# A graph attention layer on one core: pick units that run on across groups, and reciprocals that follow their roots later

## The chip, the cores and the metric

The kernel runs on one core of one Trainium2 chip. The metric is the device time of one execution in microseconds. The kernel before took 2001.13 us in the median of 3 runs, 1995.0 to 2002.62 us.

Five engines work beside each other, each in the order of its own instruction stream, and they wait for one another by semaphores: TensorE (PE in the profile, its weight loads PEld), VectorE (DVE), ScalarE (ACT), GpSimd (POOL) and SyncE (SP). Here GpSimd only issues gathers and SyncE only issues the other DMAs.

## The reference

6250 nodes with 64 features, 206250 directed edges sorted by destination. For each edge the key and value rows of its source and the query row of its destination meet with a projection of the edge's own features; messages are summed by destination, added to x, and normalised.

```python
Qh = (x @ Wq.T + bq).reshape(n, H, D)
Kh = (x @ Wk.T + bk).reshape(n, H, D)
Vh = (x @ Wv.T + bv).reshape(n, H, D)
Ee = (edge_attr @ We.T + be).reshape(-1, H, D)
score = (Kh[src] * Qh[dst] * (1.0 / np.sqrt(D)) * Ee).sum(-1)
score = jnp.exp(jnp.clip(score, -5.0, 5.0))
msg = Vh[src] * score[..., None]
wV = jax.ops.segment_sum(msg, dst, num_segments=n)
x = _layernorm(x + wV)
```

H is 4, D is 16.

## The kernel before

Edges come in 1612 tiles of 128. Eight tiles are a **group** (1024 edges); there are 202 groups, and the main loop (L1014) runs over them. Two groups are a **step**; sums of a step are made in the even group that follows it (L1079), so only every second group has them, and they are added (`add`, L893) in the odd group after that.

A group g needs five things of its neighbours in the pipeline: `edges` (L746) projects the edge features of g+3 into the PSUM tile `room`, first half; `biased` (L751) copies that to `eb` on ScalarE with the bias; `queries` (L757) spreads query rows over edges by a one-hot matrix `to` into the PSUM tile `qq`; `terms` (L765) multiplies the two on VectorE; `turn` (L771) transposes the product into `qe` on TensorE. Then `products`, `weigh` and `message` (L804, L811, L817) make scores, weights and messages, `keep` and `take` (L842, L846) split a message into two parts (`msg`), and `sums` (L865) multiplies them on TensorE with the one-hot `wide` (made by `onehot_edges`, L777, on VectorE as `of` and widened on ScalarE). The sums land in the second half of `room`.

**Where keys and values come from.** Most tiles get their rows by indirect DMA on GpSimd (`gather`, L316, one tile each). Some are picked by TensorE instead: four tiles (512 sources) are one **collection** m. A collection is 13 **units**; a unit is four matmuls of 128x512 (the last unit two) of node features `parts` with a one-hot matrix `hot`, summed in two PSUM tiles `pick` (`picks`, L709). Units come in 7 **pieces** of two (the last of one); `hots` (L688) makes the one-hot of a piece on VectorE one group ahead, pieces 1, 3 and 5 as `thin` in bf16, which ScalarE widens (L707). When the 13 units are done, `picked` (L719) reads both `pick` tiles on VectorE into `x` (L722, L723). Only then may the next collection's first unit overwrite `pick`. In the group after, `biased_kv` (L731, ScalarE) puts a bias into `qq`, `picked_kv` (L725) makes 16 matmuls on it, `place_kv` (L736, ScalarE) copies the rows out, and only after this copy can `queries` write `qq` again. `sources` (L254) prepares the next collection's indices with two ScalarE passes and one on VectorE; `fetch_sources` (L248) loads them.

Collections take 3 and 2 groups by turns. The group in which a collection ends is in `READY` (3, 5, 8, 10, 13, ...), the one in which it begins in `BEGIN`. A collection never shares a group with another: a three-group collection runs 4, 4 and 5 units, a two-group one 6 and 7. The order of all instructions is written out by hand, the loop body being that order.

At the end of blocks of 128 nodes, `roots` (L978, ScalarE: a table of functions is loaded, then a square root), `scales` (L981, VectorE: the reciprocal) and `norm` (L984) follow each other in one group, for batches that close at 16, 32, 42 and 47 blocks.

Of the kernel before, what the change touches and what calls it, by code (L numbers as in the profile page):

```python
# [97 lines left out]


def pieces_of(g):  # L100

    for m in range(LAST):
        if BEGIN[m] <= g <= READY[m]:
            n, k = READY[m] - BEGIN[m] + 1, g - BEGIN[m]
            return [(m, p) for p in range(len(PIECES) * k // n, len(PIECES) * (k + 1) // n)]
    return []

# [42 lines left out]
def tile_gnn(ctx: ExitStack, tc: tile.TileContext, x, x_blocks, by_rows, xT, wT, bias, beT, weT, eT, src, src_rows,  # L150
# [502 lines left out]
    with tc.If(rv == 0) as branch:  # L653

        with tc.tile_pool(name="work", bufs=2) as work, \
# [13 lines left out]
            folded = room[:, 1, 2 * PA:2 * PA + 2 * C].rearrange("p (b c) -> p b c", c=C)  # L669
            sum_ = still[:, 2 * P:2 * P + C]  # L670
# [310 lines left out]
            def scales(lo, hi):  # L981
                nc.vector.reciprocal(rstd[:, lo:hi], rstd[:, lo:hi])
# [12 lines left out]

            closed, scaled, normed = 0, 0, 0
            step_of = {g: s for s in range(NS) for g in groups_of(s)}
# [16 lines left out]
            for g in range(NG + 1):  # L1014
                now, before = g < NG, g > 0
                todo, ahead = [(m, p, u) for m, p in pieces_of(g) for u in range(*PIECES[p])], pieces_of(g + 1)
                going, where = [], []
# [8 lines left out]
                if g % LG == 0 and g + 3 * LG < NG:  # L1026
                    fetch_edges(g // LG + 3, work, 3)
                if g + 1 in BEGIN[1:]:
                    fetch_sources(BEGIN.index(g + 1) + 1, work)
                if g + 4 < NG:  # L1030
# [48 lines left out]
                if g - 1 in ends and now:  # L1079
# [3 lines left out]
                    else:  # L1083
                        short.append(lambda: sums(s))
                for k in range(max(len(todo), 3)):
# [11 lines left out]
                    if k in (2, 4) and short and g not in READY:  # L1097
# [5 lines left out]
                if g + 3 < NG:  # L1103
# [19 lines left out]
                if parted:  # L1123
                    take(g, 0)
                if g in READY:
                    picked(READY.index(g))
                if done:

                    while closed < B - 2 and summed[closed] <= g:
                        spreads(closed)  # L1130
                        closed += 1
                    if closed in BATCHES and closed > scaled:
                        roots(scaled, closed)
                        scales(scaled, closed)
                        scaled = closed
                    for _ in range(3):
# [185 lines left out]
```

## Time and profile before

The profiled execution took 2019.47 us, 18.3 us over the median of the runs; its span, from the first to the last instruction, is 2017.7 us.

| What | Before |
|---|---|
| median of 3 runs | 2001.13 us |
| profiled execution | 2019.47 us |
| its span | 2017.7 us |
| granted TensorE clock, mean | 0.932 |
| TensorE busy | 1738.5 us |
| VectorE busy | 1486.0 us |
| ScalarE busy | 1328.1 us |
| GpSimd busy | 1255.5 us |

A row of the groups reads: line, engine, operation, written tile and read tiles, shape, count, then busy time in all, mean ns of one, and the idle time of the engine just before these instructions with what ended it. A row of the waits reads: who waited, for whom, us in all, how often, the longest. A row of the timeline reads: start, duration, engine, line, instruction, and in brackets the idle time before it and what ended it. A row of the windows lists for a stretch the busy time of each engine and then the share of full speed that the TensorE clock was granted (PEclk). All of TensorE's products are recorded at one helper line, L744, so tiles tell them apart.

### The profile page before, as it was taken

To read this page: it belongs to the slowest core of one execution; us is meant where nothing else is said; L and a number is where in the kernel's file an instruction comes from. 1 tells how busy PE (TensorE), PEld (TensorE's weight loads), DVE (VectorE), ACT (ScalarE), POOL (GpSimd) and SP (SyncE) were. 2 spreads that over 40 slices of the span, in tenths; PEclk is the share of its full clock that TensorE was granted. 3 is DMA by queue.
4 is the path that set the end of the run, shared out by engine and by line. 5 is a ranking of instruction groups with operands and counts; after the bars stand their busy time and mean duration, and the time that the engine had idled before them with its cause. 6 is when DMAs were issued, how large, how long until landed. Compare 5 with 4: busy or idle time off the path is not lost.

```text
span 2017.7 us, 25692 instructions
## 1 busy us (share of the span) xinstructions
PE 1738.5 (86%) x7993; PEld 1259.1 (62%) x7993; DVE 1486.0 (74%) x2650; ACT 1328.1 (66%) x2047; POOL 1255.5 (62%) x1310
## 2 busy tenths in 40 slices
PE   6569989888888898979888989888888988889995
PEld 6346666666666665657566666666666666656664
DVE  5457777777777686878777777778777777678786
ACT  3456676676766676767667667667766667577674
POOL 6566666666666665666666666666666666666441
PEclk9789999999999998999899999999989999999996
DMA  6523333333333333333333333333333333333320
GB/s 178 190 90 114 100 103 103 98 97 100 93 108 101 91 102 88 102 115 99 93 97 92 107 104 93 104 90 103 101 88 114 104 95 104 97 93 98 97 71 20
DMA packets 116116, 203.70 MB, mean 101 GB/s; under 512 B 54784, under 2 KB 56425, under 8 KB 115855
## 3 DMA queue, kind: packets, MB, share of 16 engines
q1 hardware_dynamic: 73932, 116.94, 19.0%
q0 software_dynamic: 41600, 83.97, 14.7%
q10 hardware_dynamic: 436, 1.04, 0.2%
q8 instruction: 65, 1.06, 0.2%
q14 instruction: 83, 0.68, 0.1%
HBM read 194.25 MB, written 7.59 MB: 100 GB/s over the span
## 4 chain that ended last, share of the span: by engine, by line
PE 63%; DVE 16%; issue 7%; ACT 6%; another core or an unknown queue 4%; DMA 2%; POOL 1%; DVEq 0%; SPq 0%; ACTq 0%; POOLq 0%
PE pick L744 37%; PE room L744 10%; PE qq L744 10%; PE qe L775 4%; DVE hot L696 3%; DMA kv<-kv_tab,src_i 2%; DVE score L808 2%; DVE prod L806 1%; DVE qe L830 1%; DVE x L722 1%; DVE term L769 1%; POOL kv L295 1%; ACT kv L739 1%; DVE msg L850 1%
## 5 line engine op out<-in xcount | busy, mean ns | idle before, releaser
L295 POOL DMA_INDIRECT kv<-kv_tab,src_i x1260 | 1216.2, 965 | 708.8 <-issue 277.1
L744 PE MATMUL pick<-hot,parts 128*128 128x512 f32 x3900 | 1143.6, 436 | 115.5 <-DVE x L722 79.5
L744 PEld LDWEIGHTS pick<-hot,parts 128*128 128x128 f32 x3900 | 742.3, 198 | 418.8 <-issue 167.8
L696 DVE TENSOR_TENSOR hot<-from,still 128x1024 fp32r<-128x1024 bf16 x231 | 280.3, 1213 | 0.6 <-ACT from L257 0.6
L707 ACT ACTIVATE hot<-thin 128x1024 fp32r<-128x1024 bf16 x234 | 245.4, 1049 | 19.4 <-remote 19.3
L769 DVE TENSOR_TENSOR term<-eb,qq 128x512 f32<-128x512 f32 x202 | 137.3, 680 | 137.2 <-PE qq L744 98.1
L755 ACT ACTIVATE eb<-room,be_col 128x512 f32<-128x512 f32 x202 | 137.1, 679 | 148.2 <-DVE still L900 50.4
L744 PE MATMUL room<-et,we_sb 128*128 128x512 f32 x404 | 226.2, 642 | 7.5 <-ACT eb L755 6.2
L844 ACT ACTIVATE msg<-qe 128x512 fp32r<-128x512 f32 (+1 forms) x206 | 123.2, 598 | 157.5 <-DVE qe L830 74.4
L278 ACT ACTIVATE to<-to,one_p 126x1024 bf16<-126x1024 bf16 x198 | 225.7, 1140 | 0.1
L272 ACT ACTIVATE to<-kb,minus_row 126x1024 bf16<-126x1024 uint8 x198 | 225.2, 1137 | 0.0
L813 ACT ACTIVATE score<-score,five_p 128x32 f32<-128x32 f32 x203 | 64.1, 316 | 235.4 <-DVE score L808 144.6
L775 PE MATMUL qe<-ident,term 128*128 128x128 f32 x806 | 135.5, 294 | 58.9 <-DVE term L769 39.4
L775 PEld LDWEIGHTS qe<-ident,term 128*128 128x128 f32 x806 | 104.0, 151 | 111.9 <-DVE term L769 55.8
L744 PE MATMUL qq<-w,x 128*128 128x128 f32 x1248 | 165.8, 288 | 5.0 <-issue 3.6
L806 DVE TENSOR_TENSOR prod<-kv,qe 128x512 f32<-128x512 f32 x203 | 137.0, 675 | 43.1 <-remote 38.3
L830 DVE SCALAR_TENSOR_TENSOR qe<-weight,kv 128x512 f32<-128x512 f32 x200 | 139.8, 699 | 35.1 <-ACT weight L815 22.3
L722 DVE SCALAR_TENSOR_TENSOR x<-odd,upper,pick 128x512 f32<-128x512 int32 x77 | 57.3, 744 | 144.7 <-PE pick L744 115.2
L744 PEld LDWEIGHTS qq<-w,x 128*128 128x128 f32 x1248 | 155.6, 202 | 12.9 <-issue 8.0
L696 DVE TENSOR_TENSOR thin<-from,still 128x1024 bf16<-128x1024 bf16 x231 | 157.1, 680 | 0.0
L808 DVE TENSOR_REDUCE score<-prod 128x32 f32<-128x512 f32 x203 | 138.5, 682 | 7.0
L850 DVE TENSOR_TENSOR msg<-qe,msg 128x512 fp32r<-128x512 f32 x194 | 132.2, 681 | 2.9 <-ACT msg L844 1.4
(166 smaller groups left out, 1490.5 us busy)
## 6 DMA issues: line engine op xcount, KB each, us to landing
et<-in_eT SPq DMA_DIRECT2D x100, 512.0 KB
kb<-key_tab SPq DMA_DIRECT2D x101, 252.0 KB
kv<-kv_tab,src_i POOLq DMA_INDIRECT x1260
srcs<-in_src_rows SPq DMA_DIRECT2D x78, 256.0 KB
qw<-q_tab SPq DMA_DIRECT2D x202, 15.8 KB
kv_tab<-kv_sb SPq DMA_DIRECT2D x4, 640.0 KB
q_tab<-q SPq DMA_DIRECT2D x5, 480.0 KB
out<-y SPq DMA_DIRECT2D x2, 512.0 KB
```

Source lines behind the costliest of these rows:

```text
L272: nc.scalar.activation(TO[g][:, :n, :], KB.pop(g)[:, :n * P].rearrange("p (j e) -> p j e", j=n), AF.Square, bias=minus_row3[:3 * W])
L278: nc.scalar.activation(TO[g][:, :n, :], TO[g][:, :n, :], AF.Relu, bias=one_p[:3 * W], scale=-1.0)
L295: return nc.gpsimd.indirect_dma_start(out=kv_of(g)[:, j, :], out_offset=None, in_=kv_tab[:, :], in_offset=bass.IndirectOffsetOnAxis(ap=src ...
L696: nc.vector.tensor_tensor(to.rearrange("p b (a c) -> p b a c", c=2), pairs((FROM if hi < UNITS else OVER)[m])[:, None].to_broadcast(shape) ...
L707: nc.scalar.activation(*THIN.pop(0), AF.Copy)
L744: mark.append(nc.tensor.matmul(*aps, **kw))
L769: nc.vector.tensor_mul(TERM[g][:, :n], EB.pop(g)[:, :n], qq[:, :n])
L775: nc.tensor.transpose(qe[g % 2][:, 2 * k:2 * k + 2, :], TERM[g][:, k, :], ident)
L806: nc.vector.tensor_mul(prod, kv_of(g)[:, lo:hi, :C], qe[g % 2][:, lo:hi, :])
L808: nc.vector.tensor_reduce(SCORE[g], prod.rearrange("p g (h d) -> p g h d", h=H), axis=AX.X, op=OP.add)
L830: nc.vector.scalar_tensor_tensor(to.rearrange("p g (h d) -> p g h d", h=H), WEIGHT.pop(g)[:, :, :, None].to_broadcast([P, n, H, D]), LEAST ...
L850: nc.vector.tensor_sub(part_of(g, 1)[1], left, part)
```

## The change

Three things change, and the arithmetic stays the same.

1. All units of all collections are one stream, and groups take 4, 6, 6, 4, 6 units of it by turns (5 in the very first). A collection's last units now share a group with the next one's first: in a group of `READY` the **head** is what still belongs to the ending collection. It has 2 units in groups 3, 8, 13, ... (short head) and 5 in groups 5, 10, 15, ... (long head). With a short head, head and `picked` come early in the group, ahead of the one-hots; then `turn`, `queries`, `sums` and `edges`, and behind them 4 units of the next collection. With a long head, the head comes where units stood before, then `queries`, `sums`, `edges`, and behind them one unit of the next collection; `picked` stands ahead of `onehot_edges`. `sources` moves from the group after into the group of `READY`, and `fetch_sources` from the group of `READY` into the one before.
2. The PSUM tile `room` of two halves becomes two tiles: `ee` (for `edges`) and `room` (for `sums` and the folding of blocks).
3. `scales` of a batch follows `roots` two groups later (the last batch at once, as before).

```diff
+FLOW = 4, 6, 6, 4, 6
+STREAM = [(m, p, u) for m in range(LAST) for p, piece in enumerate(PIECES) for u in range(*piece)]
+UPTO = [0] * (LEAD + 1)
+for g in range(LEAD, NG):
+    UPTO.append(UPTO[-1] + FLOW[(g - LEAD) % len(FLOW)] + (g == LEAD))
...
+def units_of(g):
+
+    return STREAM[UPTO[g]:UPTO[g + 1]] if g < NG else []
...
 def pieces_of(g):
...
+    return [(m, p) for m, p, u in units_of(g) if u == PIECES[p][0]]
...
+SOURCES = {LEAD: 1, **{r: m + 2 for m, r in enumerate(READY)}}
+FETCHES = {r - 1: m + 2 for m, r in enumerate(READY)}
...
-            room = fixed.tile([P, 2, 4 * P], F32, name="room")
-            ee = room[:, 0].rearrange("p (i e) -> p i e", e=P)
-            pa = room[:, 1, :2 * PA]
+            ee = fixed.tile([P, G // 2, P], F32, name="ee")
+            room = fixed.tile([P, 4 * P], F32, name="room")
+            pa = room[:, :2 * PA]
...
+                todo, ahead = units_of(g), pieces_of(g + 1)
+                ending = READY.index(g) if g in READY else None
+                head = [one for one in todo if one[0] == ending]
...
+                if 0 < len(head) <= 3:
+                    for one in head:
+                        picks(*one)
+                        where.append(mark[-1])
+                    picked(ending)
...
+                for k, one in enumerate(head if len(head) > 3 else []):
+                    picks(*one)
+                    where.append(mark[-1])
+                    if k == 1 and g + 1 < NG:
+                        turn(g + 1)
+                if head:
+                    if len(head) <= 3 and g + 1 < NG:
+                        turn(g + 1)
+                    if g + 2 < NG:
+                        queries(g + 2)
+                    while short:
+                        short.pop(0)()
+                    if g + 3 < NG:
+                        edges(g + 3)
+                    if len(head) > 3:
+                        picked(ending)
+                    for one in todo[len(head):]:
+                        picks(*one)
+                        where.append(mark[-1])
+                for k in range(0 if head else max(len(todo), 3)):
...
-                if g in BEGIN:
-                    sources(BEGIN.index(g) + 1, *from_odd())
+                if g in SOURCES:
+                    sources(SOURCES[g], *from_odd())
...
-                if g in READY:
-                    picked(READY.index(g))
...
+                    if rooted > scaled:
+                        scales(scaled, rooted)
+                        scaled = rooted
+                    if closed in BATCHES and closed > rooted:
+                        roots(rooted, closed)
+                        rooted = closed
+                        if closed == BATCHES[-1]:
+                            scales(scaled, closed)
+                            scaled = closed
```

Three places of the built programs show it, all around group 13, a group with a short head. First TensorE, at the end of group 13 before: the last unit (two single matmuls), the edge features of group 16, and the next collection's first unit.

```order
L744 MATMUL pick_757<-hot,parts 128x512
L744 MATMUL pick_758<-hot,parts 128x512
L744 MATMUL room<-et,we_sb 128x512
L744 MATMUL pick_757<-hot,parts 128x512 x2
L744 MATMUL pick_758<-hot,parts 128x512 x2
```

And TensorE from the last unit on in the changed program; the two `pick` tiles are called pick_758 and pick_759 there.

```order
L758 MATMUL pick_758<-hot,parts 128x512
L758 MATMUL pick_759<-hot,parts 128x512
L789 MATMUL qe_763<-ident,term 128x128 x4
L758 LDWEIGHTS qw
L758 MATMUL qq<-to,qw 64x512
L758 LDWEIGHTS qw
L758 MATMUL qq<-to,qw 64x512
L758 MATMUL ee<-et,we_sb 128x512
L758 MATMUL pick_758<-hot,parts 128x512 x2
L758 MATMUL pick_759<-hot,parts 128x512 x2
```

Between the last unit of one collection and the first of the next stood `edges` alone; now `turn` (`qe`), `queries` (`qq`) and `edges` stand there.

Second VectorE in group 13 before, from the first one-hot ahead to `picked` (the two `x`); `of` is the one-hot of the sums, `msg` is `take`.

```order
L696 TENSOR_TENSOR hot<-from,still 128x1024
L830 SCALAR_TENSOR_TENSOR qe_763<-weight,kv_67 128x512
L696 TENSOR_TENSOR thin<-from,still 128x1024
L696 TENSOR_TENSOR hot<-from,still 128x1024
L792 TENSOR_TENSOR of<-still,key 128x1024
L850 TENSOR_TENSOR msg<-qe_763,msg 128x8x64
L722 SCALAR_TENSOR_TENSOR x_759<-odd,upper,pick_757 128x512
L723 SCALAR_TENSOR_TENSOR x_760<-odd,upper_82,pick_758 128x512
```

And VectorE in group 13 of the changed program:

```order
L736 SCALAR_TENSOR_TENSOR x_760<-odd,upper,pick_758 128x512
L737 SCALAR_TENSOR_TENSOR x_761<-odd,upper_82,pick_759 128x512
L710 TENSOR_TENSOR hot<-from,still 128x1024
L844 SCALAR_TENSOR_TENSOR qe_764<-weight,kv_67 128x512
L710 TENSOR_TENSOR thin<-from,still 128x1024
L273 TENSOR_SCALAR odd<-srcs 128x512
L806 TENSOR_TENSOR of<-still,key 128x1024
L864 TENSOR_TENSOR msg<-qe_764,msg 128x8x64
```

`picked` has moved from the end of the group to ahead of the first one-hot and of the message (L844); one one-hot has gone to another group and `odd` (of `sources`) has come.

Third ScalarE, with what each instruction waits for, from `biased` (`eb`) of group 13 to `biased_kv` of group 14 (the `qq` row), before:

```order
L755 ACTIVATE eb<-room,be_col 128x512 [waits DVE_49,PE_49]
L844 ACTIVATE msg<-qe_763 128x8x64 [waits DVE_49]
L272 ACTIVATE to<-kb,minus_row_86 126x1024
L707 ACTIVATE hot<-thin 128x1024 [waits DVE_49]
L278 ACTIVATE to<-to,one_p 126x1024 [waits Activation_49]
L797 ACTIVATE wide<-of 128x1024 [waits DVE_49]
L813 ACTIVATE score<-score,five_p 128x32 [waits DVE_49]
L815 ACTIVATE weight<-score,five_p 128x32 [waits Activation_49]
L733 ACTIVATE qq<-bkv_all 128x512 [waits DVE_49,PE_49]
```

And in the changed program:

```order
L769 ACTIVATE eb<-ee,be_col 128x512 [waits PE_49]
L858 ACTIVATE msg<-qe_764 128x8x64 [waits DVE_49]
L286 ACTIVATE to<-kb,minus_row_86 126x1024
L721 ACTIVATE hot<-thin 128x1024 [waits DVE_49]
L292 ACTIVATE to<-to,one_p 126x1024 [waits Activation_49]
L271 ACTIVATE from<-srcs,from_row 128x512 [waits DMAHW1_49]
L272 ACTIVATE over<-srcs,last_row 128x512
L811 ACTIVATE wide<-of 128x1024 [waits DVE_49]
L827 ACTIVATE score<-score,five_p 128x32 [waits DVE_49]
L829 ACTIVATE weight<-score,five_p 128x32 [waits Activation_49]
L747 ACTIVATE qq<-bkv_all 128x512 [waits DVE_49]
```

The wait of `eb` for VectorE is gone, and the two passes of `sources` (`from`, `over`) now stand between group 13's message and group 14's `biased_kv`; before they stood behind `place_kv` of group 14.

More of the change, by code (lines that the diff above doesn't have):

```diff
@@ L97 @@
 READY = [begin(m + 1) - 1 for m in range(LAST)]
-def pieces_of(g):
[L102 to L106, printed above, removed]
+FLOW = 4, 6, 6, 4, 6
[3 more added lines that the diff above has]
+    UPTO.append(UPTO[-1] + FLOW[(g - LEAD) % len(FLOW)] + (g == LEAD))
+assert UPTO[NG] >= len(STREAM)
+assert all(UPTO[r] < (m + 1) * UNITS <= UPTO[r + 1] for m, r in enumerate(READY))
+def units_of(g):
+    return STREAM[UPTO[g]:UPTO[g + 1]] if g < NG else []
+def pieces_of(g):
+    return [(m, p) for m, p, u in units_of(g) if u == PIECES[p][0]]
+SOURCES = {LEAD: 1, **{r: m + 2 for m, r in enumerate(READY)}}
+FETCHES = {r - 1: m + 2 for m, r in enumerate(READY)}
 PICKED = [(r + k, r + k + 1) for r in READY for k in [min(4, NG - 2 - r - 1)]]
@@ L1015, in tile_gnn @@
                 now, before = g < NG, g > 0
-                todo, ahead = [(m, p, u) for m, p in pieces_of(g) for u in range(*PIECES[p])], pieces_of(g + 1)
+                todo, ahead = units_of(g), pieces_of(g + 1)
+                ending = READY.index(g) if g in READY else None
+                head = [one for one in todo if one[0] == ending]
                 going, where = [], []
@@ L1027, in tile_gnn @@
                     fetch_edges(g // LG + 3, work, 3)
-                if g + 1 in BEGIN[1:]:
-                    fetch_sources(BEGIN.index(g + 1) + 1, work)
+                if g in FETCHES:
+                    fetch_sources(FETCHES[g], work)
                 if g + 4 < NG:
@@ L1084, in tile_gnn @@
                         short.append(lambda: sums(s))
-                for k in range(max(len(todo), 3)):
+                for k, one in enumerate(head if len(head) > 3 else []):
[18 more added lines that the diff above has]
+                for k in range(0 if head else max(len(todo), 3)):
                     for one in todo[k:k + 1]:
@@ L1096, in tile_gnn @@
                             queries(g + 2)
-                    if k in (2, 4) and short and g not in READY:
+                    if k in (2, 4) and short:
                         short.pop(0)()
@@ L1102, in tile_gnn @@
                     queries(g + 2)
-                if g + 3 < NG:
+                if g + 3 < NG and not head:
                     edges(g + 3)
```

8 lines of the change are left out of this document (2 added, 6 removed).

## The prediction

> **What bounds the kernel now.** I read the page first: the engines' shares, the chain that ended last, and the two largest groups of instructions.
>
> ```profile
> PE 1738.5 (86%) x7993; PEld 1259.1 (62%) x7993; DVE 1486.0 (74%) x2650; ACT 1328.1 (66%) x2047; POOL 1255.5 (62%) x1310
> ...
> PE 63%; DVE 16%; issue 7%; ACT 6%; another core or an unknown queue 4%; DMA 2%; POOL 1%; DVEq 0%; SPq 0%; ACTq 0%; POOLq 0%
> ...
> L295 POOL DMA_INDIRECT kv<-kv_tab,src_i x1260 | 1216.2, 965 | 708.8 <-issue 277.1 <-PE pick L744 198.6 <-PE room L744 76.5
> L744 PE MATMUL pick<-hot,parts 128*128 128x512 f32 x3900 | 1143.6, 436 | 115.5 <-DVE x L722 79.5 <-issue 35.1
> ```
>
> TensorE is busy for 86% of the span and is 63% of the chain, so the time is TensorE's work plus its idle time (2017.7 - 1738.5 = 279 us) plus what a lower clock adds to the work. GpSimd, 1216.2 us busy and 277.1 us between its own issues, has some 500 us to spare: it is no bound for what follows. Next the waits of TensorE, in us in all, times, and the longest.
>
> ```profile
> PE pick L744 <- DVE x L722: 79.5, 23, 6.0
> ...
> PE qq L744 <- ACT kv L739: 44.0, 32, 4.4
> ...
> PE qe L775 <- DVE term L769: 39.4, 22, 12.3
> ...
> PE pick L744 <- issue: 35.1, 37, 2.5
> ...
> PE qe L775 <- DVE score L808: 10.2, 2, 5.1
> ```
>
> The largest is the one that the change goes at: a collection's first unit waits for `picked` of the one before. The timeline of a group in which a three-group collection ends shows how it comes about.
>
> ```profile
> 992.23 1.02 PE L744 MATMUL room<-et,we_sb 128*128 128x512 f32 x2
> ...
> 992.73 0.68 DVE L769 TENSOR_TENSOR term<-eb,qq 128x512 f32<-128x512 f32 x1
> ...
> 995.82 2.59 PE L744 MATMUL pick<-hot,parts 128*128 128x512 f32 x10
> ...
> 995.98 0.64 DVE L900 TENSOR_REDUCE still<-room 64x64 f32<-64x128 f32 x2 [2.56 <-PE qq L744]
> ...
> 996.71 0.69 ACT L755 ACTIVATE eb<-room,be_col 128x512 f32<-128x512 f32 x1 [2.77 <-DVE still L900]
> ...
> 998.25 1.02 PE L744 MATMUL room<-et,we_sb 128*128 128x512 f32 x2
> 998.28 0.70 DVE L830 SCALAR_TENSOR_TENSOR qe<-weight,kv 128x512 f32<-128x512 f32 x1
> ...
> 999.49 1.22 DVE L696 TENSOR_TENSOR hot<-from,still 128x1024 fp32r<-128x1024 bf16 x1
> ...
> 1001.82 0.74 DVE L722 SCALAR_TENSOR_TENSOR x<-odd,upper,pick 128x512 f32<-128x512 int32 x1
> ```
>
> TensorE is through with this group's short work at 999.3; VectorE, held for 2.56 us ahead of `add` and then busy with three one-hots, comes to `picked` only at 1001.82. And behind it:
>
> ```profile
> 1002.61 3.78 PE L744 MATMUL pick<-hot,parts 128*128 128x512 f32 x8 [3.34 <-DVE x L722]
> ...
> 1004.57 0.32 ACT L813 ACTIVATE score<-score,five_p 128x32 f32<-128x32 f32 x1 [0.99 <-issue]
> ...
> 1005.22 0.60 ACT L733 ACTIVATE qq<-bkv_all 128x512 f32<-128x512 f32 x1
> ...
> 1006.19 1.05 PE L775 MATMUL qe<-ident,term 128*128 128x128 f32 x4
> ```
>
> The eight matmuls after the wait take 3.78 us where ten took 2.59 before it: the clock has fallen. The windows of 7 us behind six of these waits (first and last shown; PEclk is the last number but two) have 0.60, 0.76, 0.68, 0.60, 0.76 and 0.76 of the clock, mean 0.69.
>
> ```profile
> 1002.60:1009.60 7.00, 6.99 (x30) 6.03 (x31) 6.97 (x12) 5.98 (x10) 5.48 (x6) 0.60 0.25 75
> ...
> 1768.60:1775.60 7.00, 7.00 (x34) 5.79 (x34) 6.96 (x12) 5.98 (x10) 5.47 (x6) 0.76 0.27 77
> ```
>
> **The change part by part.** *The wait for `picked`.* In a short-head group TensorE begins with 2 units, 6 matmuls at 2.59/10 = 0.26 us, done at 1.5 us. VectorE then needs two passes of 0.74, so `pick` is free at some 3.0. Meanwhile TensorE does `turn` (about 0.5), `queries` (0.4) and `edges` (1.0), and asks for `pick` at 3.4: the wait is gone with 0.4 to spare. With a long head it asks at some 1.4 (no sums) to 2.5 us (sums) after the head, and its first two matmuls need the first pass alone (0.74): gone too. I take all of the 79.5 us; the other end is that half of it comes back, 40, where signals are as late as the 2.56 us ahead of `add`. The clock behind these waits: 7 us at 0.69 lose 2.15 us, and about 20 of the 23 are long enough, so 42 us; at the other end 20.
>
> *The split of `room`.* `eb` no longer waits for VectorE (2.77 us above). That is ScalarE's idle time ahead of a message that it waits for anyway, so I count nothing for it; at best it helps what I work out next, and it costs nothing, the instructions being the same.
>
> *The reciprocals.* VectorE stands still until ScalarE has loaded a table and taken the root, and TensorE stands behind it.
>
> ```profile
> 798.02 1.12 PE L775 MATMUL qe<-ident,term 128*128 128x128 f32 x4 [4.48 <-DVE term L769]
> ...
> 1423.87 1.28 ACT L979 ACT_TABLE_LOAD   x1
> ...
> 1425.51 0.25 DVE L982 RECIPROCAL rstd<-rstd 128x16 f32<-128x16 f32 x1 [3.19 <-issue]
> ...
> 1428.52 1.11 PE L775 MATMUL qe<-ident,term 128*128 128x128 f32 x4 [5.07 <-DVE score L808]
> ```
>
> Three batches do this in the loop (the two waits of 10.2 us above and the 4.48 of 798.02, where the reciprocal is just as late); two table loads of 1.28 stay on ScalarE. I take 4 us, and 2 us of clock as above, from each: 18 us; bounds 0 and 25.
>
> *What is late next.* In a short-head group `picked` now stands ahead of the one-hot and the message on VectorE, and behind the message ScalarE has a long queue, to which `sources` is added. The rows of its parts, mean ns after the busy time:
>
> ```profile
> L707 ACT ACTIVATE hot<-thin 128x1024 fp32r<-128x1024 bf16 x234 | 245.4, 1049 | 19.4 <-remote 19.3
> L278 ACT ACTIVATE to<-to,one_p 126x1024 bf16<-126x1024 bf16 x198 | 225.7, 1140 | 0.1
> L272 ACT ACTIVATE to<-kb,minus_row 126x1024 bf16<-126x1024 uint8 x198 | 225.2, 1137 | 0.0
> ...
> L844 ACT ACTIVATE msg<-qe 128x512 fp32r<-128x512 f32 (+1 forms) x206 | 123.2, 598 | 157.5 <-DVE qe L830 74.4 <-issue 50.9 <-DVE hot L696 28.7
> ...
> L797 ACT ACTIVATE wide<-of 128x1024 fp32r<-128x1024 bf16 x97 | 101.7, 1048 | 0.0
> ...
> L257 ACT ACTIVATE from<-srcs,from_row 128x512 bf16<-128x512 int32 x77 | 55.5, 720 | 0.0
> ```
>
> From the group's start: `pick` read at 3.0, one one-hot (1.22), message (0.70) to 4.8; then ScalarE 0.60 + 1.14 + 1.05 + 1.14 + 2 x 0.72 + 1.05 (`wide`, in odd groups only) = 6.4, some 0.1 less each since they overlap, so 5.7: to 10.5. Then `score`, `weight` (0.32 each) and `biased_kv` (0.60): 11.7. TensorE is through at 3.4 + 16 x 0.26 = 7.5, and in the next group after two units (2.0) and `turn` at 10.0, where it wants `biased_kv` for the 16 matmuls of `picked_kv`. So a **new wait of 1.7 to 2.0 us** stands there. In even groups `wide` is missing and TensorE has the sums (about 1.1) more: no wait. Of 39 short heads half are odd: 19 x 2.0 = 38 us; bounds 0 and 39 x 3.34 = 130, a wait as long as today's behind every short head. It makes its own fall of the clock. The nearest row is a wait of 2.08 us for `place_kv`:
>
> ```profile
> 1079.86 0.64 PE L744 MATMUL qq<-to,qw 126*64 126x512 bf16 x2 [2.08 <-DMA kb<-key_tab]
> ...
> 1079.80:1083.30 3.50, 3.44 (x7) 1.76 (x7) 1.82 (x2) 3.47 (x7) 2.02 (x3) 0.51 0.21 61
> ```
>
> Half clock for 3.5 us, 1.7 us lost. Not each wait of this length will do so; I take half, 19 x 1.7 / 2 = 16 us (bounds 0 and 32). The Trainium skill, TensorE: Matmul & The Clock Gate, section HAM oscillation — how this bites in real kernels, has the rule that idle gaps of over about 3.4 us throttle the clock. By that rule the new waits would cost no clock and the sum would be 16 us better; this trace does not quite agree, with 2.08 us of idle time at half clock.
>
> *`place_kv`.* Behind a short head the next group has four units now and had six, so less work covers `place_kv` ahead of `queries`; but the 44.0 us hold such waits as that of 1079.86, in a group behind a two-group collection, which had four units and still has. Even groups keep sums between them, and the wait for `biased_kv` above pushes both sides equally. Unchanged; bounds -10 and +25. *Signals that come late* at the 39 short heads (TensorE then waits for `eb` or `pick`): 0 to 1.1 each; 0.3, so 12 us. *Moved DMAs*: `fetch_sources` comes one group earlier on SyncE, ahead of that group's queries and keys, as it stood in its old group; nothing. The one-hots are as many as before, spread 2, 3, 3, 2, 4 over the groups; nothing.
>
> **The sum**, against the profiled execution of 2019.5: -79.5 - 42 - 18 + 38 + 16 + 12 = -73.5, so 1946. The median of the runs lies 18.3 us under that execution, so **1928 us**.
>
> **The rivals.** *All of it stays (no new wait).* If ScalarE, freed of the 2.77 us, keeps pace, the three costs fall away: 2001 - 139.5 = 1862. For it: ScalarE is busy for 66% only. Against: it is busy exactly behind the message. Chance 0.17.
>
> *The wait moves in full.* It costs nothing in sum when each short head brings 139.5/39 = 3.6 us of waits and clock. Then 2001, within 0.5%, which is about what a measurement of this kernel can tell from no change. It is also what comes if VectorE is late as it is today and the unit behind the head waits for `picked` as before. Chance 0.10.
>
> *Slower.* VectorE, in order, stands at `picked` until the head is done, and everything behind it, message, one-hots and next products, slides; ScalarE's queue with it, in even groups too. If each of the 39 short heads brings a wait at `picked_kv` as long as today's (3.34) with its clock (2.15), that is 39 x 5.5 = 214 us against 139.5 gained: 2076. It decides from 3.6 us a head on; I worked out 2.0 in one of two, and ScalarE would have to be 2.8 us later than that in even groups. Chance 0.12.
>
> **How the numbers follow.** My forecast has 0.61, the rivals 0.17, 0.10 and 0.12. Faster by over 0.5%: 0.61 + 0.17 = 0.78; within: 0.10; slower: 0.12. The range goes down to the case in which all of it stays, 1862, and up over the case in which nothing does, 2003; above it I leave the slower case, and some little below.
>
> **What would show it.** In the profile after, the wait of `pick` for `x` should fall from 79.5 to under 20 us, and VectorE's wait for a root from 10.3 to nearly nothing; a wait of `qq` for ScalarE's bias should appear behind short heads of odd groups, 1 to 3 us each; the mean clock should rise from 0.932 by about 0.02. I am wrong in the step on ScalarE's queue if that wait is missing or stands behind even groups too, and wrong in the first step if `pick` still waits for `x`.

## The result, and the profile after

The changed kernel takes 2013.63 us in the median of 13 runs (2000.46 to 2019.84), the kernel before 1999.15 us beside it (13 runs, 1991.77 to 2005.81): ratio 1.0066, interval 1.0047 to 1.0084. It is slower by 0.66%; the prediction was 1928 us, 3.6% faster.

One thing must be said first, since numbers below can't be read without it. The runs came in six sittings, each with the kernel before beside it on the same chip. In four of them the kernel before took 1999 to 2018 us, in two 1786 us. What tells their traces apart is this: in the first kind, TensorE's semaphore signals often come late. Counted from the semaphore updates of a trace, some 300 signals of before, and as many of after, came over 1 us behind the end of the matmul that gives them; in the second kind 0 to 2. I call the two kinds **late** and **on time**. The chip alone does not decide it: a late sitting and one on time, 44 minutes later, ran on a chip of the same number. All ratios are within a sitting.

Of the page of after: the engines' busy time, the chain that ended last, and three groups of instructions, in which the old and the new waits stand.

```profile
PE 1714.0 (85%) x7993; PEld 1253.8 (62%) x7993; DVE 1485.9 (74%) x2650; ACT 1324.9 (66%) x2047; POOL 1259.7 (63%) x1310
...
PE 51%; ACT 17%; DVE 14%; issue 10%; another core or an unknown queue 3%; DMA 2%; SPq 1%; POOL 0%; DVEq 0%; ACTq 0%; POOLq 0%
...
L758 PE MATMUL pick<-hot,parts 128*128 128x512 f32 x3900 | 1111.7, 430 | 24.2 <-issue 14.5
...
L858 ACT ACTIVATE msg<-qe 128x512 fp32r<-128x512 f32 (+1 forms) x206 | 122.6, 595 | 263.2 <-DVE qe L844 130.9
...
L758 PE MATMUL qq<-to,qw 126*64 126x512 bf16 x396 | 84.1, 417 | 108.0 <-ACT kv L753 79.8
```

The idle time ahead of `pick` has fallen from 115.5 to 24.2 us, but TensorE's share of the chain fell from 63% to 51% and ScalarE's rose from 6% to 17%. TensorE's waits in after:

```profile
PE qq L758 <- ACT kv L753: 79.8, 37, 5.5
PE qe L789 <- DVE term L783: 43.5, 30, 6.0
PE qq L758 <- ACT qq L747: 35.5, 25, 2.2
...
PE qq L758 <- DMA kb<-key_tab: 11.8, 6, 2.7
PE pick L758 <- DVE x L736: 8.9, 8, 1.8
...
PE qe L789 <- DVE score L822: 8.3, 7, 1.8
...
PE qq L758 <- DMA qw<-q_tab: 5.4, 1, 5.4
```

Beside them the same view of a second profiled execution of the unaltered kernel before, which ran in a later sitting with late signals and had a span of 2003.6 us:

```profile
PE pick L744 <- DVE x L722: 81.5, 25, 5.2
PE qe L775 <- DVE term L769: 38.6, 18, 9.3
PE qq L744 <- ACT kv L739: 35.6, 25, 3.0
```

And the engines' row of its page:

```profile
PE 1730.4 (86%) x7993; PEld 1251.7 (62%) x7993; DVE 1485.5 (74%) x2650; ACT 1327.1 (66%) x2047; POOL 1248.6 (62%) x1310
```

The first profiled execution of before (span 2017.7) was longer than any of its 13 timed runs, so the second is the better neighbour of after (2011.8). Against it TensorE is busy for 16.4 us less (1730.4 to 1714.0) and idle for 24.6 us more (273.2 to 297.8): +8.2. The wait for `x` has gone (81.5 to 8.9, -72.6). In its place stand `biased_kv` (+35.5), `place_kv` (+44.2), and key and query rows from DMA (17.2; 4.4 in the trace beside it, but only 3.4 in the second trace of after, so this part is not steady). **The wait moved in full, and somewhat more.**

The timeline of after shows the two places. Behind an odd short head:

```profile
988.94 0.75 DVE L736 SCALAR_TENSOR_TENSOR x<-odd,upper,pick 128x512 f32<-128x512 int32 x1 [3.85 <-PE ee L758]
...
991.57 0.70 DVE L844 SCALAR_TENSOR_TENSOR qe<-weight,kv 128x512 f32<-128x512 f32 x1
...
997.99 0.31 ACT L827 ACTIVATE score<-score,five_p 128x32 f32<-128x32 f32 x1
...
998.56 0.58 ACT L747 ACTIVATE qq<-bkv_all 128x512 f32<-128x512 f32 x1
...
999.19 2.05 PE L758 MATMUL qq<-w,x 128*128 128x128 f32 x16 [2.18 <-ACT qq L747]
```

VectorE stands at `picked` for 3.85 us with the message behind it; ScalarE gets the message at 992.3, comes to `biased_kv` at 998.56, and TensorE waits 2.18 us. That is the wait that the prediction worked out. Behind an even short head it counted none. For the bias that holds (all such waits there make 4.6 us), but one step later, at `place_kv`, stands another:

```profile
1043.20 2.05 PE L758 MATMUL qq<-w,x 128*128 128x128 f32 x16
...
1045.01 2.11 PE L758 MATMUL pick<-hot,parts 128*128 128x512 f32 x8
...
1051.90 0.66 ACT L753 ACTIVATE kv<-qq 128x256 f32<-128x256 f32 x2 [4.78 <-remote]
...
1052.61 0.64 PE L758 MATMUL qq<-to,qw 126*64 126x512 bf16 x2 [5.49 <-ACT kv L753]
```

The 16 matmuls of `picked_kv` end at 1045.25. ScalarE is free from 1047.12 on, but the signal reaches it only at 1051.9, 6.6 us after the end. The two units behind `picked_kv` are through at 1047.12, and TensorE stands for 5.49 us. Where six units stood in this group before, four (16 matmuls, 4.2 us) covered this way. Counted by place, 48.3 of the 79.8 us for `place_kv` stand behind even short heads, 30.0 behind long heads and 1.6 behind odd short heads; in the first trace of before it was 12.1 behind even three-group collections and 32.0 behind two-group ones. Behind an odd short head the sums (1.12 us at 1003.86) stand between `picked_kv` and `queries` too; behind an even one only the two units do.

### The profile page after: what moved, and what is told of

Read it like the earlier page. It is cut to its first block, busy times and chain, and to the rows that moved or that the text cites. A ratio compares the mean times of both kernels' runs of the same rounds, so it can differ in the third digit from the quotient of the medians.

```text
span 2011.8 us, 25666 instructions
## 1 busy us (share of the span) xinstructions
PE 1714.0 (85%) x7993; PEld 1253.8 (62%) x7993; DVE 1485.9 (74%) x2650; ACT 1324.9 (66%) x2047; POOL 1259.7 (63%) x1310
## 4 chain that ended last, share of the span: by engine, by line
PE 51%; ACT 17%; DVE 14%; issue 10%; another core or an unknown queue 3%; DMA 2%; SPq 1%; POOL 0%; DVEq 0%; ACTq 0%; POOLq 0%
PE pick L758 28%; PE qq L758 8%; PE ee L758 8%; PE room L758 4%; ACT hot L721 4%; PE qe L789 3%; DVE hot L710 2%; ACT to L286 2%; DVE x L737 2%; ACT msg L858 2%; ACT to L292 2%; DVE score L822 1%; DVE prod L820 1%; PE ps L527 1%
## 5 line engine op out<-in xcount | busy, mean ns | idle before, releaser
L758 PE MATMUL pick<-hot,parts 128*128 128x512 f32 x3900 | 1111.7, 430 | 24.2 <-issue 14.5
L758 PE MATMUL ee<-et,we_sb 128*128 128x512 f32 x404 | 236.5, 669 | 9.2 <-ACT eb L769 6.8
L769 ACT ACTIVATE eb<-ee,be_col 128x512 f32<-128x512 f32 x202 | 136.6, 676 | 140.4 <-PE ee L758 44.3
L758 PE MATMUL qq<-w,x 128*128 128x128 f32 x1248 | 177.8, 302 | 41.9 <-ACT qq L747 35.5
L758 PEld LDWEIGHTS qq<-w,x 128*128 128x128 f32 x1248 | 163.9, 212 | 54.6 <-ACT qq L747 44.0
L789 PE MATMUL qe<-ident,term 128*128 128x128 f32 x806 | 126.2, 280 | 75.9 <-DVE term L783 43.5
L758 PE MATMUL qq<-to,qw 126*64 126x512 bf16 x396 | 84.1, 417 | 108.0 <-ACT kv L753 79.8
L789 PEld LDWEIGHTS qe<-ident,term 128*128 128x128 f32 x806 | 97.0, 143 | 123.5 <-DVE term L783 60.9
L844 DVE SCALAR_TENSOR_TENSOR qe<-weight,kv 128x512 f32<-128x512 f32 x200 | 139.9, 699 | 39.6 <-issue 14.1
```

The source lines that it names most:

```text
L758: mark.append(nc.tensor.matmul(*aps, **kw))
L789: nc.tensor.transpose(qe[g % 2][:, 2 * k:2 * k + 2, :], TERM[g][:, k, :], ident)
L844: nc.vector.scalar_tensor_tensor(to.rearrange("p g (h d) -> p g h d", h=H), WEIGHT.pop(g)[:, :, :, None].to_broadcast([P, n, H, D]), LEAST ...
```

## The experiments

Theories, as the runs name them. A: ScalarE's queue is late because the message waits on VectorE behind `picked`. B: too few units cover the way over `place_kv`. C: whatever TensorE gains comes back as the next wait. D: the gain is there where signals are on time. E: the wait for `x` is itself large only where they are late.

### The message ahead of `picked`

```diff
-                    picked(ending)
                 if g - 1 in READY:
...
                 if now:
                     message(g, *some_of(g)[0])
+                if 0 < len(head) <= 3:
+                    picked(ending)
```

> The changed kernel, but in a group with a short head VectorE takes the first one-hot and the message ahead of `picked`, not behind it. Theory A (ScalarE's queue is late because the message is held back on VectorE while `picked` waits for the head): ScalarE's wait for the message falls from 130.9 us to some 75 (74.4 in the kernel before), TensorE's wait for `biased_kv` from 35.5 us to under 10, its wait for `place_kv` by some of its 79.8; together 25 to 60 us less than the changed kernel, a ratio to the kernel before of 0.976 to 0.994 (changed kernel: 1.0066). Theory B (the wait for `place_kv` comes from the four units, where six covered it, and not from the message): the bias wait may go, 35.5 us at most, `place_kv` stays at 80. Theory C (whatever TensorE gains in these groups is given back in the next wait): the waits change their names and the ratio stays within 0.003 of 1.0066.

Measured: 1.0044 (1.0025 to 1.0064), signals late. Its waits:

```profile
PE qq L758 <- ACT kv L753: 95.7, 41, 6.4
...
PE pick L758 <- DVE x L736: 21.3, 13, 5.5
```

The wait for `biased_kv` is nearly gone (0.7 us), as A said; but `place_kv` has 15.9 us more and `x` 12.4. A was right about the cause of that one wait and wrong about the time; C comes nearest.

> The changed kernel with the message ahead of `picked`, unaltered from its run of 1.0044. Where signals are on time: theory A: the wait for `biased_kv` (32.6 us in the changed kernel) goes, and with it the fall of the clock behind it, 35 to 50 us, ratio 0.966 to 0.974, so that the order on VectorE alone explains most of what the run with 4, 5, 6, 6, 5 units had (0.9613); theory B: without the six units it keeps over half of the way to 0.9613, 0.977 to 0.99. Where signals are late: 1.0044 within 0.004.

Signals were late again: 1.0048 (1.0029 to 1.0066).

### Five units behind the short head

```diff
-FLOW = 4, 6, 6, 4, 6
+FLOW = 4, 6, 5, 5, 6
```

> The changed kernel with 4, 6, 5, 5, 6 units: one unit moves from the group with the short head to the group behind it, where it stands after `picked_kv` and covers `place_kv` (four matmuls of 0.26 us, 1.04 us). Theory B: the wait for `place_kv` falls from 79.8 us by up to 1.04 x 38 = 40, at least by 20; the ratio falls from 1.0066 to 0.987 to 0.997. Theory A: `biased_kv` is asked for 1.04 us sooner and its wait grows by about 19 x 1.04 = 20 us, so what the one wait loses the other gains: 1.0066 within 0.004.

Measured: 1.0058 (1.0031 to 1.0085), signals late. Its waits:

```profile
PE qq L758 <- ACT kv L753: 55.7, 29, 5.2
...
PE qq L758 <- ACT qq L747: 30.3, 20, 2.2
...
PE qq L758 <- ACT score L827: 9.4, 5, 2.2
PE qq L758 <- ACT weight L829: 9.0, 6, 2.2
```

`place_kv` lost 24.1 us, as B said, but the time is A's (1.0066 within 0.004). For `biased_kv` is wanted sooner: with `score` and `weight`, which stand directly ahead of it on ScalarE, its way has 48.7 us of waits (39.4 in after). Counted by place, TensorE now also waits for the bias behind even short heads (16.4 us), where it had waited for 4.6.

### Both at once

> The changed kernel with the message ahead of `picked` and with 4, 6, 5, 5, 6 units: between the two others, five units behind the short head. Where signals are on time: by theory A the same as without the fifth unit, by theory B halfway to 0.9613. Where signals are late: between 1.0044 and 0.9986, with 50 to 75 us of waits for `place_kv`.

Measured, signals late: **0.9965** (0.9942 to 0.9987), better than either bound that was written down. Its waits:

```profile
PE qq L758 <- ACT kv L753: 69.3, 30, 5.3
...
PE pick L758 <- DVE x L736: 18.7, 16, 3.1
...
PE qq L758 <- ACT qq L747: 6.1, 11, 1.0
```

Either edit alone is worth 0.1 to 0.2%, which the intervals leave open, both together 1.0%, which is clear of them. Behind a short head stand two waits in series: for `biased_kv`, and after two units for `place_kv`. An edit that shortens one hands TensorE sooner to the other: with the message first, the wait for `place_kv` behind odd short heads grew from 1.6 to 17.4 us, and with five units that for the bias behind even ones from 4.6 to 16.4. The two (with `score` and `weight`) held 89 us behind short heads in after, 62 with the message first, 66 with five units, 27 with both.

### Six units behind the short head, message first

```diff
-FLOW = 4, 6, 6, 4, 6
+FLOW = 4, 5, 6, 6, 5
```

> The changed kernel with the message ahead of `picked` (as in the run before, 1.0044) and with 4, 5, 6, 6, 5 units, so that six units stand behind a short head as in the kernel before: eight matmuls of 0.26 us more cover `place_kv`, and `biased_kv` is asked for after one unit less in the group ahead. Theory B: of the waits for `place_kv` behind short heads in the run before (44.8 and 17.4 us) some 40 go, ratio about 0.985. Theory A: the bias wait, which the earlier message had removed, comes back with 10 to 20 us, as one unit less stands ahead of it. Theory C: 1.004 within 0.004, with the waits in other places.

With these numbers a short head has three units instead of two, and a long one four instead of five. This sitting had signals on time: 1716.03 us, **0.9613** (0.9598 to 0.9627), better than any of the three theories had it. TensorE is busy for 95% of the span; its waits:

```profile
PE qe L789 <- DVE term L783: 45.1, 35, 6.0
PE qq L758 <- ACT kv L753: 9.0, 19, 0.7
...
PE qq L758 <- ACT qq L747: 0.4, 2, 0.2
```

Both waits behind short heads are gone (the 9.0 us stand behind long heads), and A's return of the bias did not come.

> The changed kernel with the message ahead of `picked` and with 4, 5, 6, 6, 5 units, unaltered from its run of 0.9613. Without late signals: 0.961 within 0.002. With late signals: theory B about 0.985; theory C 1.004 within 0.004; theory D says that with two units more of cover behind the short head fewer ways round meet a late signal, 0.98 to 0.995.

With late signals: 0.9986 (0.9968 to 1.0005), between D's range and C's. `place_kv` has 51.6 us, most of it now behind long heads, and `x`, which had 8.9 in after, 47.8: with late signals the waits come back on other ways round.

### `edges` ahead of `queries`

```diff
-                if g + 2 < NG and g - 1 in READY:
-                    queries(g + 2)
                 if g + 3 < NG and not head:
                     edges(g + 3)
+                if g + 2 < NG and g - 1 in READY:
+                    queries(g + 2)
```

> The changed kernel, with one difference: in the groups behind a finished collection, `edges` (two matmuls, 1.02 us) stands ahead of `queries` on TensorE, so that it lies beside the way from the last matmul of `picked_kv` over `place_kv` back to `queries`. Theory B (what is missing is work that covers this way, two units where four stood): each of the 37 waits for `place_kv` gets up to 1.02 us shorter, 79.8 us become 42 to 55, and the time falls by 25 to 38 us, ratio 0.988 to 0.994 (changed kernel: 1.0066). Theory C (each wait that goes comes back as another): the wait for `place_kv` falls as well, but waits for `term` and for the bias grow by as much, and the ratio stays at 1.0066 within 0.004.

Signals on time: 0.9821 (0.9807 to 0.9834). Below B's range, which had been written for late signals; the changed kernel has 0.9933 in this condition (below), so the edit is worth 1.1%; `place_kv` has 10.4 us with it and 28.4 without.

> The changed kernel with `edges` ahead of `queries` behind a finished collection, unaltered from its run of 0.9821. Without late signals: 0.982 within 0.002, and the difference to the changed kernel of this call is what the edit is worth (theory B: the 19 and more waits for `place_kv`, 10 to 40 us). With late signals: theory B 0.988 to 0.994, theory C 1.0066 within 0.004, as written for its first run.

With late signals: 1.0022 (1.0005 to 1.004), the changed kernel 1.0061 beside it: between B's range and C's. Of its waits:

```profile
PE qe L789 <- DVE term L783: 60.9, 41, 6.0
PE qq L758 <- ACT kv L753: 40.0, 20, 4.6
```

The changed kernel's own trace in this sitting has 79.5 for `kv` and 34.9 for `term`. `place_kv` falls by what B said, and `queries`, now 1 us later, makes `term` late, as C said: 39.5 us taken, 26.0 given back.

> The kernel of the run before it (message first, 4, 5, 6, 6, 5 units) with `edges` ahead of `queries` as well. Theory B: the two gains add up but for what the units cover already, ratio 0.972 to 0.985. Theory C: 1.004 within 0.004.

On time: 0.9755 (0.9742 to 0.9769), worse than without `edges` first (0.9613). Where six units cover the way already, the edit has little to take (9.0 us for `place_kv`), and `term` comes late: 62.7 us against 45.1. That is not all of the 25 us: TensorE is idle for 13.4 us more and busy for 11.9 more (1626.2 to 1638.1), and no run explains the second part.

> The changed kernel with the message ahead of `picked`, with 4, 5, 6, 6, 5 units and with `edges` ahead of `queries` behind a finished collection, unaltered from its run of 0.9755. Where signals are on time: 0.9755 within 0.002, so worse than without the last edit (0.9613). Where they are late: the run without `edges` first had 0.9986 and 51.6 us of waits for `place_kv`; theory B: some 20 of them go, 0.985 to 0.992; theory C: 0.9986 within 0.004.

On time once more: 0.9737 (0.9724 to 0.9751).

> The kernel before with its own order of units, with `ee` and `room` apart and late reciprocals (0.9968 in its run), and with `edges` ahead of `queries` behind a finished collection. Its waits for `place_kv` were 40.1 us, 28 of them, most behind two-group collections. Theory B: up to 1.02 us each, 20 to 28 us, ratio 0.983 to 0.987. Theory C: 0.997 within 0.003, with the wait of `pick` for `x` grown from 88.3 us by what the other lost.

On time: 0.9972 (0.9961 to 0.9984). That is C's number. What the edit took here cannot be read off, since neither the kernel before nor its two small parts alone were traced on time; 8.9 us for `place_kv` are what is left with it. Its waits say more:

```profile
PE qe L775 <- DVE term L769: 53.1, 66, 6.0
PE pick L744 <- DVE x L722: 31.3, 21, 2.4
PE qq L744 <- ACT kv L739: 8.9, 15, 0.6
```

With the old order of units and signals on time, the wait for `x` is 31.3 us, where late runs of this order with the two small parts have 68.6 to 92.6.

### The two small parts

The changed kernel with the reciprocals at once again:

```diff
-                    if rooted > scaled:
-                        scales(scaled, rooted)
-                        scaled = rooted
-                    if closed in BATCHES and closed > rooted:
-                        roots(rooted, closed)
-                        rooted = closed
-                        if closed == BATCHES[-1]:
-                            scales(scaled, closed)
-                            scaled = closed
+                    if closed in BATCHES and closed > scaled:
+                        roots(scaled, closed)
+                        scales(scaled, closed)
+                        scaled = closed
```

> The changed kernel with the reciprocals directly behind their roots again. If the late reciprocals are worth what the prediction said (18 us, bounds 0 and 25), this is 18 us longer than the changed kernel: a ratio of about 1.016 to the kernel before, with VectorE's wait for a root back at 10 us and one TensorE wait of 4 to 5 us at each of three batches. If they are worth nothing, 1.0066 again, within 0.003.

Measured: 1.0097 (1.0073 to 1.0121), signals late: 0.0031 over the changed kernel, some 6 us, with intervals that overlap. And the kernel before with parts 2 and 3 alone (`ee` and `room` as two tiles, `scales` two groups later, as in the change's diff):

> The kernel before with `ee` and `room` as two tiles and with the reciprocals two groups behind their roots, and with its own order of units. If these two parts are worth what the prediction said (nothing and 18 us): a ratio of 0.991, bounds 0.9875 and 1. If the split lets `eb` start up to 2.8 us sooner and that reaches TensorE (which waits for `term` for 39.4 us in all), up to 20 us more: 0.981. If one of them does harm: above 1.003, and then the units are worth more than the changed kernel shows.

> The kernel before with `ee` and `room` apart and the reciprocals two groups behind their roots, unaltered from its run of 0.9968. Without late signals: if the two parts are worth the same, 0.997 within 0.002; if the split matters only where signals are late (the eviction then waits for VectorE), 1.000 within 0.002. With late signals: 0.9968 within 0.003.

> The kernel before with `ee` and `room` apart and the reciprocals two groups behind their roots, unaltered from 0.9968 and 0.9974. Where signals are on time: 0.997 within 0.002 if the parts are worth the same there, 1.000 within 0.002 if they matter only where signals are late; `edges` first would then be worth what is left to 0.9972. Where signals are late: 0.997 within 0.003.

Measured, all three with late signals: 0.9968 (0.9953 to 0.9982), 0.9974 (0.9957 to 0.9991), 0.9964 (0.9944 to 0.9984). The two parts gain 0.3%, some 6 us (0.991 was expected), of which the reciprocals explain all that can be told apart. On time they were not tried alone. So the stream of units by itself **costs** 1.0066 / 0.9968, 1.0%, where signals are late.

### The two kernels unaltered

> The kernel before itself, unaltered, for its trace. Ratio 1.000 within 0.002. Where signals are on time: the run of this order of units with the two small parts and `edges` first had 31.3 us of waits of `pick` for `x` (21 of 1.5 us), so theory E (the wait that the change removes is itself 80 us only where signals are late, and some 30 us where they are on time) has 25 to 35 us here; the prediction's row of 79.5 us would say 80. Where signals are late: 70 to 90 us by both.

Signals late: 0.9999 (0.998 to 1.0017), 81.5 us for `x`. No trace of before itself was had with signals on time, so E rests on the run of the kernel before with `edges` first.

> The changed kernel itself, unaltered. In the four runs with 4, 5, 6, 6, 5 units or `edges` first, the kernel before took 1786.5 us where it took 1998.7 us in the four runs ahead of them, and their traces show hardly a late signal of TensorE (2, 1 and 0 by over 1 us, against 291 in the trace of before). Where it runs without late signals (kernel before at some 1786): theory D (the change gains where signals are on time, and what eats it is the late signals, which each short way round over ScalarE now meets) 0.985 to 0.993, as the run with `edges` first had 0.982 and 10.4 us of waits for `place_kv`, and lacks only that edit; theory C 1.0066 within 0.004 here too. Where it runs with late signals (kernel before at some 1999): 1.0066 again by both.

Signals late: 1.0061 (1.0035 to 1.0087).

> The changed kernel itself, unaltered. Where TensorE's signals are on time (kernel before at some 1786 us): theory D 0.985 to 0.993, theory C 1.0066 within 0.004. Where they are late (kernel before at some 2000): 1.0066 within 0.004 by both.

Signals on time: 1773.6 against 1785.81 us, **0.9933** (0.9919 to 0.9947), at the edge of D's range (0.985 to 0.993). Its waits:

```profile
PE qe L789 <- DVE term L783: 42.3, 34, 6.0
PE qq L758 <- ACT qq L747: 32.6, 20, 2.1
PE qq L758 <- ACT kv L753: 28.4, 19, 1.7
```

And its timeline at the place of the program that stood at 1043.20 above:

```profile
916.55 2.05 PE L758 MATMUL qq<-w,x 128*128 128x128 f32 x16
...
918.36 2.11 PE L758 MATMUL pick<-hot,parts 128*128 128x512 f32 x8
...
919.48 0.65 ACT L753 ACTIVATE kv<-qq 128x256 f32<-128x256 f32 x2
...
920.40 0.41 PE L758 MATMUL qq<-to,qw 126*64 126x512 bf16 x2
```

On time, `kv` is copied at 920.13 and TensorE goes on without a gap: two units are just enough, and all 28.4 us stand behind long heads. The bias wait is there in full, 20 waits of 1.6 us: what TensorE no longer waits for `x` (31, if the run with `edges` first stands for the kernel before) it waits for the bias (32.6). Where the 0.7% that the change still gains comes from is open; the small parts may have a share, but were not tried alone on time.

## Why the prediction was wrong

**The step that failed** is that on `place_kv`: "four units now and had six, so less work covers `place_kv` [...] Unchanged; bounds -10 and +25". The wait was 44.0 before (35.6 in the second trace) and is 79.8 after (79.5 in the second): 36 to 44 us instead of none, above the upper bound. The step saw the missing cover and argued it away with a group that has four units too, without working out the slack. What it said of two-group collections is right (32.0 us before, 30.0 behind long heads after), and so is that even groups keep their sums between; but behind every second short head, the even ones, two units are all that is left, and there 12.1 us became 48.3. The run with five units shows that the cover is what is missing (17.1 there), and `edges` first that other work does as well (31.5, against 56.2 in the changed kernel beside it). On time the same two units are just enough, with no wait for `place_kv` behind any short head. So the step failed for want of slack against late signals, which the prediction counted for `eb` and `pick` only, at 12 us in all.

The sum said -73.5; against the second trace of before +8.2 was measured, 82 us apart. `place_kv` is the largest piece of that; the others follow.

**The wait for `x`, -79.5**: gone where signals are late (8.9 left in after; 26.6 in the second trace of it). But the price was read from one trace. It was some 3.4 us each; on time, in the run with the old order of units and `edges` first, it is 1.5 us each, 31 in all, so over half of it seems to be late signals. The prediction had the row that told of it, VectorE held for 2.56 us ahead of `add`, until 995.98, though the sums had ended at 992.39, and counted such signals only at the 39 short heads, 12 us.

**`biased_kv`, +38**: right, 35.5 late and 32.6 on time (19 waits of 2.0 forecast, 20 of 1.6 measured on time), nearly all of it behind short heads of odd groups (30.2 late, all on time).

**The clock**: -42 + 16, with some -6 of the roots. TensorE's busy time fell by 24.5 us against the first trace, 16.4 against the second, and the mean clock rose from 0.932 to 0.945 (0.02 forecast). Right in sign, too large by a quarter to a half. The new waits slow the clock as well: of 42 stretches at half clock in each trace, 19 began at a wait for `x` and 4 at one for `place_kv` in the first trace of before; in after it is 2 and 12, and 7 at the bias.

**The reciprocals, -18**: the two waits of 5 us for `score` are gone (the longest is 1.8), but the time says some 6 us.

**The split of `room`, nothing**: no run contradicts it.

**The rivals.** In its mechanism "the wait moves in full" (2001) came nearest, by another way than it was argued: 1.8 us per short head of new waits at the bias and `place_kv` (35.5 + 35.8 over 39) were enough, not 3.6, as clock and reciprocals brought less. In its number, 0.66% is past the 0.5% that was set as its limit: that is the slower case, at a small part of its size. The slower rival expected the wait at `picked_kv` in even groups too; there it hardly stands (4.6 us), the new one being at `place_kv`, and its price of 5.5 per head was too high.

## What to carry to other kernels

Before work is moved away from behind a hand-over, write down the slack of each way round that stays there: from the last matmul over the other engine back to TensorE, against the work that covers it; here two waits stood in series, and with late signals shortening one was worth 0.1 to 0.2%, shortening both 1.0%. A stall that vanishes pays only what is not waiting right behind it. And a wait's price from one trace holds for that condition alone: the same change is 0.66% slower where signals are late and 0.67% faster where they are on time, and the version with the message first and six units is 3.9% faster there and no different (0.9986) where they are late.

## What the runs showed of the hardware

**Late signals.** On time, an idle engine starts at a nearly fixed delay after the end of the matmul that it waits for, as the trace has that end: in the third trace of the changed kernel the medians are 0.04 us for `x` and `eb`, 0.10 for `kv` and 0.11 for `term`, and of 184 such waits only one is over 0.15 (0.47, a `term`). In the trace of after, the same delays go up to 5.2 us for `x`, 7.0 for `eb`, 6.7 for `kv` and 5.6 for `term`. The updates then come in bunches: in after, the next one behind 1045.36 is at 1050.40, another at 1051.82, and three more within 0.14 us of that. At 1041.48 ten updates begin that lie within 0.40 us, while one matmul of a unit takes 0.24 us just there (20 in 4.84 us at 1037.80): so the signals are held back and not only the matmuls late. Many updates are missing from late traces (1717 of 2167 are there in before, 2393 of 2405 in the third trace of the changed kernel), which is why the count of late ones is rough. VectorE and ScalarE run on meanwhile, as long as they need nothing of TensorE. No group of instructions and no DMA queue of the trace of after starts clearly more often just ahead of these stretches than elsewhere (the largest difference is 65% against 54%), so their cause stays open. They are what divides 1786 from some 2000 us as far as the traces show; no run took them away by itself.

**The clock falls after short waits, for fixed stretches.** In the third trace of the changed kernel, with signals on time, one of the bias waits in the timeline:

```profile
1044.67 2.70 PE L758 MATMUL qq<-w,x 128*128 128x128 f32 x14 [2.13 <-ACT qq L747]
```

The windows behind this wait and behind another, and an undisturbed one (PEclk is the last number but two):

```profile
1045.40:1048.80 3.40, 3.40 (x15) 3.19 (x15) 3.37 (x6) 3.20 (x6) 2.16 (x3) 0.50 0.49 143
1212.60:1216.00 3.40, 3.40 (x15) 3.01 (x14) 3.06 (x5) 3.40 (x6) 2.09 (x3) 0.51 0.41 107
...
780.00:783.40 3.40, 3.40 (x16) 2.52 (x14) 3.37 (x8) 3.40 (x5) 2.49 (x4) 1.00 0.43 152
```

In the loop of this trace half clock lasts 3.4 us, once 6.8, and 11 of its stretches stand at bias waits of 0.6 to 2.1 us. The Trainium skill, TensorE: Matmul & The Clock Gate, section HAM oscillation — how this bites in real kernels, has the rule that idle gaps of over about 3.4 us throttle the clock. This trace does not agree: 2.13 us sufficed. Not each such wait does it: 20 waits, 11 stretches, which is the half that the prediction took without a reason. The trace shows one: all half-clock stretches of the loop begin on a grid of 3.413 us, to within 0.003. From 80 to 1729 us of the span, TensorE was idle for 1.72 us or more in each of the 14 cells of that grid that were followed by half clock (11 of them with a bias wait), and for 1.67 us at most in the 455 others that ran at full clock. So a wait of 2.1 us counts if it lies in one cell and does not if it falls across two. With late signals the two sets nearly part in the same place (1.63 and more, 1.82 and less in after).
